# Layer 0's last tile: the work behind a recurrence, done by quarters of the tokens beside it

## The chip, the cores and the metric

The kernel runs on one NeuronCore of a Trainium2 chip. The metric is device time in microseconds (us) for one execution. The core has five engines that this text names as the profile does: PE (matmuls; PEld is its weight loads), DVE (VectorE), ACT (ScalarE), POOL (GpSimd) and SP (SyncE, which issues most DMAs). They run side by side and wait for one another on semaphores; each works its own queue in order.

## The reference, cut to what matters

Four layers, each an attention-like part and a feed-forward part, run over 8 sequences of 512 tokens with 128 channels. The change is in the first part of layer 0, a recurrence with 16 heads of 8 channels. After projections have made r, w, k, v, kk, b (and a gate g) for every token, it computes for each sequence and head:

```python
def step(S, inp):
    r_, w_, k_, v_, kk_, b_ = inp
    sab = jnp.einsum('bhvk,bhk->bhv', S, kk_)
    S = S * jnp.exp(w_)[:, :, None, :] + sab[..., None] * b_[:, :, None, :] + v_[..., None] * k_[:, :, None, :]
    y = jnp.einsum('bhvk,bhk->bhv', S, r_)
    return (S, y)
...
mu = y.mean(-1, keepdims=True)
var = ((y - mu) ** 2).mean(-1, keepdims=True)
yn = (y - mu) / jnp.sqrt(var + 0.00064) * ln_w.reshape(H, N) + ln_b.reshape(H, N)
bonus = (r4 * k4 * time_faaaa.reshape(H, N)).sum(-1, keepdims=True) * v4
out = (yn + bonus).reshape(B, T, C) * g
return out @ output.T
```

So behind the recurrence each token's eight channels of a head are normalized (mean, variance, weight and bias), a bonus is added, and the result is gated and projected.

## The kernel before, in words

Layer 0 walks the 512 tokens in four tiles of 128 (`jt` 0 to 3). In the recurrence a partition stands for one sequence and head (8 x 16 = 128). Two tokens are taken together as a pair, so a tile has `HT` = 64 pairs. The loop over `o` takes them in eight steps of `SH` = 8 pairs. In each step DVE builds `Z` (L734 to L738), then does eight time steps of ten small instructions (L747 to L759; each works on half of the value rows, so that the two halves hide each other's latency), and then multiplies the states with r into `HR` (L761 to L765). Those ten instructions depend on each other from one time step to the next.

`HR` still has to be summed over eight elements. `outputs` does this on PE: `eighths` multiplies by the identity eight times into one PSUM tile `pa` (all of it is at L364), and ACT copies the sum to its part of `Y` (L691). The call for a step stands one step later. `HR`, like `Hs`, has two buffers.

When all eight steps are done, the work behind the recurrence goes over the whole tile at once, on 128 x 1024 elements:

- DVE adds to the first token of each pair its own value times `kr` (L772, L773).
- PE sums `Y` over the eight channels (L364), and DVE makes 8 Y minus the sum (L777).
- ACT squares it into `t3` (L778), PE sums the squares (L364), ACT takes Ln and then Exp of -0.5 times that (L779, L780), which is the inverse root. ACT loads a function table ahead of each of the two.
- DVE makes V times bonus in `t3` (L781) and scales `Y` (L782), and ACT applies weight and bias, one channel at a time (eight instructions at L784).
- PE turns `Y` and `t3` together back to tokens (L796), DVE gates (L799), PE turns and projects (L804, L808) and, in the last tile, DVE multiplies by the feed-forward part and adds the residual (L813, L814).

Beside the recurrence of a tile runs other work: `coming` (projections and transposes of the next tile; there is none in the last) and `side` (the experts of the feed-forward part, which end in the last tile). In the last tile's steps 4 to 7 the feed-forward result comes back from memory (`f_d`), goes through Silu (L719), and is combined with the residual of the first three tiles (L721, L722).

The order of PE's queue is as written in the code. The order of DVE, ACT, POOL and SP is a scheduler's, which places instructions by its own estimates when the program is built. So an instruction of DVE may stand between two of the recurrence, wherever the scheduler thought that its inputs would be there.

The pool `bp` has one buffer for a name unless told otherwise, so a second tile of one name waits until the readers of the first are done.

Of the kernel before, what the change touches and what calls it, by code (L numbers as in the profile page):

```python
# [10 lines left out]
F32 = mybir.dt.float32  # L11
# [3 lines left out]
AF = mybir.ActivationFunctionType  # L15
ALU = mybir.AluOpType
# [4 lines left out]
P = 128  # L21
B = 8
T = 512
C = 128
N = B * T
NT = N // P
JT = T // P
# [45 lines left out]
def bc(ap, axis, n):  # L73

    a = ap.unsqueeze(axis)
    shape = list(a.shape)
    shape[axis] = n
    return a.to_broadcast(shape)
# [252 lines left out]
def layer0(k, x, A, at):  # L331

    nc, tc = k.nc, k.tc
# [3 lines left out]
    with ExitStack() as ctx:  # L337
# [15 lines left out]
        HT = P // 2  # L353
        s = x
# [5 lines left out]
        def eighths(src):  # L360

            ps = k.pa(src.shape[:2])
            for i in range(8):
                nc.tensor.matmul(ps, k.ident, src[:, :, i], start=(i == 0), stop=(i == 7))  # L364
            return ps
# [323 lines left out]
        def outputs(HR, y):  # L689

            nc.scalar.copy(y, eighths(HR.rearrange("p t s v n -> p (t s v) n")))  # L691

        for jt in range(JT):
            G, KE, BK, Vs, Rs, bonus, kr = ready
            coming = ahead(jt + 1) if jt + 1 < JT else iter(())
            made = None

            def go_on(n):
                nonlocal made
                for _ in range(n):  # L700
                    try:
                        next(coming)
                    except StopIteration as end:
                        made = end.value or made
            Y = bp.tile([P, P, 8], F32, name="Y")
            yp = Y.rearrange("p (t s) v -> p t s v", s=2)
            last = None
            for o in range(0, HT, SH):
                if jt == JT - 1 and o // SH >= HT // SH - JT:

                    j = o // SH - (HT // SH - JT)
                    if j < JT - 1:
                        f = fp.tile([P, B, C], F32, name=("Vt", "KNt", "Bt")[j])
                    else:
                        f = hp.tile([P, 3, 4, C], F32, name="sg").rearrange("p a b c -> p (a b) c")[:, 0:B, :]
                    old = fp.tile([P, B, C], F32, name="Gt", bufs=2)
                    nc.sync.dma_start(f, f_d.rearrange("(b j p) c -> j p b c", j=JT, p=P)[j])
                    nc.sync.dma_start(old, A["x"].rearrange("(b j p) c -> j p b c", j=JT, p=P)[j])
                    nc.scalar.activation(f, f, AF.Silu)  # L719
                    if j < JT - 1:  # L720
                        nc.vector.tensor_tensor(f, f, s_v[:, :, j, :], ALU.mult)  # L721
                        nc.vector.tensor_tensor(s_v[:, :, j, :], f, old, ALU.add)  # L722
                    else:
                        held = f, old
                next(side, None)
                go_on(3)
                if last:
                    outputs(*last)
                next(side, None)
                go_on(2)  # L730

                Z = up.tile([P, SH, 4, 8, 8], F32, name="Z", bufs=1)
                for i in range(2):
                    nc.vector.tensor_tensor(  # L734
                        Z[:, :, 3 - i], bc(Vs[:, o : o + SH, i, :], 3, 8), bc(BK[:, 1, o : o + SH, i, :], 2, 8),
                        ALU.mult,
                    )
                nc.vector.tensor_tensor(Z[:, :, 3], Z[:, :, 3], Z[:, :, 2], ALU.add)  # L738

                Hs = up.tile([P, SH, 8, 8], F32, name="Hs")  # L740
                halves = [(h, slice(h * 4, h * 4 + 4)) for h in range(2)]
                for t in range(SH):
                    prev = carry if t == 0 else Hs[:, t - 1]
                    z = Z[:, t]
                    sab = bp.tile([P, 2, 2, 4], F32, name="sab", bufs=3)
                    for h, v in halves:
                        nc.vector.tensor_tensor(  # L747
                            z[:, 0:3, v, :], bc(prev[:, v, :], 1, 3), bc(KE[:, o + t, 0:3, :], 2, 4), ALU.mult
                        )
                    for h, v in halves:  # L750
                        nc.vector.tensor_reduce(sab[:, h], z[:, 0:2, v, :], AX.X, ALU.add)
                    for h, v in halves:
                        nc.vector.tensor_tensor(
                            z[:, 0:2, v, :], bc(sab[:, h], 3, 8), bc(BK[:, 0, o + t], 2, 4), ALU.mult
                        )
                    for h, v in halves:
                        nc.vector.tensor_tensor(z[:, 0:2, v, :], z[:, 0:2, v, :], z[:, 2:4, v, :], ALU.add)
                    for h, v in halves:
                        nc.vector.tensor_tensor(Hs[:, t, v, :], z[:, 0, v, :], z[:, 1, v, :], ALU.add)  # L759
                HR = up.tile([P, SH, 2, 8, 8], F32, name="HR")  # L760
                nc.vector.tensor_tensor(HR[:, 0, 0], carry, bc(Rs[:, o, 0, :], 1, 8), ALU.mult)  # L761
                nc.vector.tensor_tensor(
                    HR[:, 1:, 0], Hs[:, 0 : SH - 1], bc(Rs[:, o + 1 : o + SH, 0, :], 2, 8), ALU.mult
                )
                nc.vector.tensor_tensor(HR[:, :, 1], Hs, bc(Rs[:, o : o + SH, 1, :], 2, 8), ALU.mult)  # L765
                carry = Hs[:, SH - 1]
                last = HR, Y[:, o * 2 : (o + SH) * 2, :].rearrange("p t v -> p (t v)")
            outputs(*last)
            go_on(40)
            ready = made  # L770
            t3 = fp.tile([P, B, C], F32, name="EWt").rearrange("p b (h n) -> p (b h) n", n=8)
            nc.vector.tensor_tensor(t3[:, 0:HT], Vs[:, :, 0, :], bc(kr, 2, 8), ALU.mult)  # L772
            nc.vector.tensor_tensor(yp[:, :, 0, :], yp[:, :, 0, :], t3[:, 0:HT], ALU.add)  # L773


            mu = bp.tile([P, P], F32, name="mu")
            nc.vector.scalar_tensor_tensor(Y, Y, 8.0, bc(eighths(Y), 2, 8), ALU.mult, ALU.subtract)  # L777
            nc.scalar.activation(t3, Y, AF.Square)  # L778
            nc.scalar.activation(mu, eighths(t3), AF.Ln, bias=k.eps_gn, scale=1.0 / 8)  # L779
            nc.scalar.activation(mu, mu, AF.Exp, scale=-0.5)  # L780
            nc.vector.tensor_tensor(t3, Vs.rearrange("p t s n -> p (t s) n"), bc(bonus, 2, 8), ALU.mult)  # L781
            nc.vector.tensor_tensor(Y, Y, bc(mu, 2, 8), ALU.mult)  # L782
            for n in range(8):
                nc.scalar.activation(  # L784
                    Y[:, :, n], Y[:, :, n], AF.Identity, scale=cn["ln_w"][:, n : n + 1], bias=cn["ln_b"][:, n : n + 1]
                )

            YT = fp.tile([P, B, C], F32, name="Rt")
            oTs = fp.tile([P, B, P], F32, name="Kt")
            yv = YT.rearrange("p b (h n) -> p n (b h)", n=8)  # L790
            gv = G.rearrange("p b (h n) -> p n (b h)", n=8)
            for n0 in range(0, 8, 4):
                ps = k.pa((P, 4, P))
                for i in range(4):
                    for src in (Y, t3):
                        nc.tensor.matmul(  # L796
                            ps[:, i, :], src[:, :, n0 + i], k.ident, start=(src is Y), stop=(src is t3)
                        )
                nc.vector.tensor_tensor(yv[:, n0 : n0 + 4, :], ps, gv[:, n0 : n0 + 4, :], ALU.mult)  # L799
            for b0 in range(0, B, 4):  # L800
                oT = oTs[:, b0 : b0 + 4, :]
                ps = k.pa((P, 4, P))
                for i in range(4):
                    nc.tensor.transpose(ps[:, i, :], YT[:, b0 + i, :], k.ident)  # L804
                nc.scalar.copy(oT, ps)
                ps = k.pa((P, 4, C))
                for i in range(4):
                    nc.tensor.matmul(ps[:, i, :], oT[:, i, :], cn["output"], start=True, stop=True)  # L808
                if jt < JT - 1:
                    nc.scalar.copy(s_v[:, b0 : b0 + 4, jt, :], ps)  # L810
                else:
                    f, old = (a[:, b0 : b0 + 4, :] for a in held)
                    nc.vector.tensor_tensor(f, ps, f, ALU.mult)  # L813
                    nc.vector.tensor_tensor(s_v[:, b0 : b0 + 4, jt, :], f, old, ALU.add)  # L814
# [1542 lines left out]
```

## Time and profile before

| | us |
|---|---|
| median of 3 runs | 3589.2 |
| lowest, highest | 3583.16, 3598.02 |
| the profiled execution | 3592.12 |
| its span, from the first to the last instruction | 3590.4 |
| mean granted PE clock, as a share of full speed | 0.861 |
| DVE busy in the span | 2323.1 |
| end of the last tile's recurrence (end of its last L765) | 838.05 |
| end of layer 0 (the last L814) | 874.98 |

A row of the timeline has start, duration, engine, line, operation, output and inputs, shapes and count; in brackets stands how long the engine had been idle before, and what ended that. A row of the windows has, for a stretch, the busy time of each engine with the number of instructions, and the clock that PE was granted. One fp32 matmul is two MATMUL records (two passes), each with its weight load. ACT's table loads have rows of their own.

### The profile page before, as it was taken

The numbers are of one execution on the slowest core, as the hardware profiler recorded it, in microseconds if no ns is written. First come the engines' busy times: TensorE is split into PE (matmuls) and PEld (weight loads), VectorE is DVE, ScalarE is ACT, GpSimd is POOL, SyncE is SP. The second block draws the span as 40 slices with busy tenths as digits, with TensorE's granted clock in tenths as the row PEclk, the third lists the DMA queues.
The fourth block names the chain that finished last, engine by engine and source line by source line (L and its number), as shares of the span: only waits on it lengthen the run. The fifth ranks groups of instructions, "written<-read, shape, count | busy, mean of one in ns | idle before, by whom it ended". The sixth has DMA issues, their size and how long they took to land.

```text
span 3590.4 us, 46304 instructions
## 1 busy us (share of the span) xinstructions
PE 2891.0 (81%) x16950; PEld 1591.5 (44%) x16950; DVE 2323.1 (65%) x6354; ACT 1793.6 (50%) x3386; POOL 733.4 (20%) x845
## 2 busy tenths in 40 slices
PE   6175868635998799698888888898789888888887
PEld 4154656534444454334434333443334444454453
DVE  7999888896583334534454554554577767777776
ACT  4173646422444355243545454455466556566655
POOL 0012131300124553211111111111112122222221
PEclk8587889766789999898999999999788888888888
DMA  4012121211001222100000000000000000000000
GB/s 121 2 30 44 32 52 32 43 49 48 1 13 35 40 42 27 45 1 1 1 1 1 1 1 1 1 1 1 21 1 1 4 1 4 4 1 7 4 1 6
DMA packets 67522, 64.59 MB, mean 18 GB/s; under 512 B 5344, under 2 KB 59616, under 8 KB 66784
## 3 DMA queue, kind: packets, MB, share of 16 engines
q1 hardware_dynamic: 39264, 42.75, 3.9%
q0 software_dynamic: 19712, 14.69, 3.1%
q10 hardware_dynamic: 8320, 4.19, 0.4%
q8 instruction: 133, 2.18, 0.2%
q14 instruction: 93, 0.76, 0.1%
HBM read 43.80 MB, written 17.83 MB: 17 GB/s over the span
## 4 chain that ended last, share of the span: by engine, by line
PE 36%; DVE 14%; ACT 10%; issue 2%; POOL 1%; DMA 0%; POOLq 0%; ACTq 0%; DVEq 0%
PE pu L1462 6%; PE ph L1443 5%; PE pu L2102 4%; DVE nm L2104 3%; PE pf L2132 2%; ACT at L2107 2%; PE pf L1511 2%; ACT at L1498 2%; ACT L1498 2%; DVE mpad L1477 1%; PE pa L1565 1%; PE pa L2145 1%; PE pu L1474 1%; PE pa L1596 1%; PE pa L2034 1%
## 5 line engine op out<-in xcount | busy, mean ns | idle before, releaser
L2107 ACT ACTIVATE at<-pu,nm 128x512 f32<-128x512 f32 x512 | 347.7, 690 | 226.8 <-DVE nm L2104 225.3
L2102 PE MATMUL pu<-qT,kT 32*128 32x512 f32 x1024 | 296.3, 740 | 79.3 <-ACT at L2107 79.1
L2104 DVE TENSOR_REDUCE nm<-pu 128x1 f32<-128x512 f32 x512 | 318.7, 680 | 39.6 <-PE pu L2102 39.2
L199 POOL TENSOR_SCALAR_AFFINE_SELECT at<-at 128x512 f32<-128x512 f32 x184 | 124.4, 676 | 1029.2 <-ACT at L1498 879.7
L1477 DVE TENSOR_REDUCE mpad<-pu 128x2 f32<-128x1024 f32 (+3 forms) x256 | 198.9, 818 | 151.1 <-PE pu L1474 151.0
L1128 ACT ACTIVATE at<-pu,rsqrt 128x1024 f32<-128x1024 f32 (+3 forms) x256 | 190.9, 792 | 188.2 <-PE pu L1123 164.1
L1443 PE MATMUL ph<-hid,f 128*128 128x512 f32 x512 | 256.9, 629 | 11.6 <-ACT hid L1444 11.5
L1498 ACT ACTIVATE at<-pu 128x1024 f32<-128x1024 f32 (+3 forms) x256 | 167.1, 701 | 163.6 <-PE pu L1462 162.5
L364 PE MATMUL pa<-HR,ident 128*128 128x128 f32 x512 | 127.4, 417 | 140.3 <-DVE HR L765 140.3
L2102 PEld LDWEIGHTS pu<-qT,kT 32*128 32x128 f32 x1024 | 100.2, 209 | 178.4 <-ACT at L2107 159.4
L364 PEld LDWEIGHTS pa<-HR,ident 128*128 128x128 f32 x512 | 112.4, 265 | 150.1 <-DVE HR L765 74.7
L2132 PE MATMUL pf<-at,va 128*32 128x512 f32 x1024 | 161.3, 708 | 11.9 <-POOL va L2119 11.9
L608 POOL DMA_INDIRECT f_d<-ys,idx x48 | 90.3, 1881 | 382.2 <-ACT ys L607 352.8
L1462 PE MATMUL pu<-kT,qT 32*128 32x512 f32 (+3 forms) x1024 | 136.2, 504 | 30.4 <-ACT at L1498 29.6
L1443 PEld LDWEIGHTS ph<-hid,f 128*128 128x128 f32 x512 | 94.8, 200 | 114.1 <-issue 90.1
L1462 PE MATMUL pu<-qT,kT 32*128 32x512 f32 (+3 forms) x1024 | 128.1, 496 | 20.3 <-DVE mpad L1477 19.9
L1123 PE MATMUL pu<-qT,kT 32*128 32x512 f32 (+3 forms) x1024 | 131.4, 519 | 5.8 <-ACT at L1128 4.9
L2119 POOL TENSOR_TENSOR va<-V,sm 128x32 f32<-128x32 f32 x128 | 34.5, 270 | 488.8 <-DVE sm L2118 428.6
L1066 POOL DMA_INDIRECT f_d<-ys,idx x64 | 103.4, 1616 | 135.1 <-DMA f_d<-ys,idx 86.1
L1498 ACT ACT_TABLE_LOAD x66 | 84.7, 1283 | 90.1 <-PE pu L1462 89.3
L1133 DVE TENSOR_TENSOR at<-at,ceiling 128x512 f32<-128x512 f32 x72 | 49.9, 694 | 106.5 <-ACT at L1128 102.5
L691 ACT COPY Y<-pa 128x128 f32<-128x128 f32 x32 | 8.4, 263 | 208.4 <-PE pa L364 208.4
(621 smaller groups left out, 6806.2 us busy)
## 6 DMA issues: line engine op xcount, KB each, us to landing
w<-in_w_dram SPq DMA_DIRECT2D x24, 512.0 KB
f_d<-zeros ACTq DMA_DIRECT2D x8, 512.0 KB, 5.7
xn_d<-xn SPq DMA_DIRECT2D x8, 512.0 KB, 3.2
w<-in_w_dram SPq DMA_DIRECT2D x16, 256.0 KB, 2.9
w<-in_w_dram SPq DMA_DIRECT2D x24, 128.0 KB, 2.1
f<-in_f_dram SPq DMA_DIRECT2D x1, 2888.0 KB
xn<-in_x_dram SPq DMA_DIRECT2D x4, 512.0 KB, 7.1
Gt<-in_x_dram SPq DMA_DIRECT2D x4, 512.0 KB, 5.0
```

Source lines behind the costliest of these rows:

```text
L199: self.nc.gpsimd.affine_select(a, a if src is None else src, pattern, ALU.is_ge, 0.0, base=0, channel_multiplier=-1)
L364: nc.tensor.matmul(ps, k.ident, src[:, :, i], start=(i == 0), stop=(i == 7))
L1123: nc.tensor.matmul(pu[:, n, 0:m], q["kT"][r, g // 2, kc * P : kc * P + P], q["qT"][r, g, kc * P :], start=True, stop=True,)
L1128: nc.scalar.activation(at_[:, i : i + 2, 0:m], pu[:, :, 0:m], AF.Square, bias=k.rsqrt2, scale=32.0**-0.5)
L1443: nc.tensor.matmul(ps, fn[n][:, c0 : c0 + P], src[:, i, :], start=(i == 0), stop=(i == 3))
L1462: self.k.nc.tensor.matmul(pu[:, n, 0:m], a[r, c0 : c0 + P], b[r, q0 : q0 + m], start=True, stop=stop)
L1477: nc.vector.tensor_reduce(top[:, i : i + 2, 16 + g % 2], pu[:, :, 0:m], AX.X, ALU.max)
L1498: nc.scalar.activation(at_[:, i : i + 2, 0:m], pu[:, :, 0:m], AF.Exp, scale=8.0**-0.5)
L2102: nc.tensor.matmul(pu, q["kT"][r, kc * P : (kc + 1) * P], q["qT"][r, g, :], start=True, stop=True)
L2104: nc.vector.tensor_reduce(nm[:, n : n + 1], pu, AX.X, ALU.max, negate=True)
L2107: nc.scalar.activation(E[:, n, :], pu, AF.Exp, bias=nm[:, w], accum_out=sm[:, w])
L2132: nc.tensor.matmul(po[i * 32 : i * 32 + 32, :], va[:, kc, c0 : c0 + 32], E[:, i, :], start=(kc == 0), stop=(kc == JT - 1))
```

## The change

In the last tile alone, the part from L772 to L784 is replaced by a generator `settle(c)` for each quarter `c` of the tile (16 pairs, 32 tokens). It has five steps, with a `yield` between them. A new quarter is begun every second step of the loop over `o`, as soon as its two `HR` have been summed; each quarter that has been begun takes one step in each further step of the loop, ahead of the sums of the last `HR`. The fourth quarter is begun after the loop, where all that is left is worked off in turns. V times bonus is written into `Vs` itself, so that L796 reads `Vs` in place of `t3`. Two tiles are new in `bp`, `square` (128 x 32 x 8) and `root` (128 x 32), with one buffer each. Tiles 0 to 2 go as before.

```diff
+            def settle(c, Y=Y, yp=yp, Vs=Vs, bonus=bonus, kr=kr):
+                pr, tk = slice(c * 16, c * 16 + 16), slice(c * 32, c * 32 + 32)
+                square = bp.tile([P, 32, 8], F32, name="square")
+                own_v = square[:, 0:16, :]
+                nc.vector.tensor_tensor(own_v, Vs[:, pr, 0, :], bc(kr[:, pr], 2, 8), ALU.mult)
+                nc.vector.tensor_tensor(yp[:, pr, 0, :], yp[:, pr, 0, :], own_v, ALU.add)
+                yield
+                y = Y[:, tk, :]
+                mean = eighths(y)
+                yield
+                nc.vector.scalar_tensor_tensor(y, y, 8.0, bc(mean, 2, 8), ALU.mult, ALU.subtract)
+                nc.scalar.activation(square, y, AF.Square)
+                v = Vs.rearrange("p t s n -> p (t s) n")[:, tk, :]
+                nc.vector.tensor_tensor(v, v, bc(bonus[:, tk], 2, 8), ALU.mult)
+                yield
+                r = bp.tile([P, 32], F32, name="root")
+                nc.scalar.activation(r, eighths(square), AF.Ln, bias=k.eps_gn, scale=1.0 / 8)
+                nc.scalar.activation(r, r, AF.Exp, scale=-0.5)
+                yield
+                nc.vector.tensor_tensor(y, y, bc(r, 2, 8), ALU.mult)
+                for n in range(8):
+                    nc.scalar.activation(
+                        y[:, :, n], y[:, :, n], AF.Identity, scale=cn["ln_w"][:, n : n + 1], bias=cn["ln_b"][:, n : n + 1]
+                    )
+                yield
+            settling = []
...
+                for w in settling:
+                    next(w, None)
                 next(side, None)
                 go_on(3)
                 if last:
                     outputs(*last)
+                    if jt == JT - 1 and o // SH % 2 == 0:
+                        settling.append(settle(o // SH // 2 - 1))
+                        next(settling[-1])
...
             outputs(*last)
+            if jt == JT - 1:
+                settling.append(settle(3))
             go_on(40)
             ready = made
+            added = Vs.rearrange("p t s n -> p (t s) n")
+            if jt == JT - 1:
+                while settling:
+                    settling = [w for w in settling if next(w, False) is not False]
+            else:
...
+                added = t3
...
-                    for src in (Y, t3):
+                    for src in (Y, added):
```

More of the change, by code (lines that the diff above doesn't have):

```diff
@@ L768, in layer0 @@
             outputs(*last)
+            if jt == JT - 1:
+                settling.append(settle(3))
             go_on(40)
             ready = made
[L771 to L786, printed above, removed]
+            added = Vs.rearrange("p t s n -> p (t s) n")
@@ new lines, in layer0 @@
+            if jt == JT - 1:
+                while settling:
+                    settling = [w for w in settling if next(w, False) is not False]
+            else:
+                t3 = fp.tile([P, B, C], F32, name="EWt").rearrange("p b (h n) -> p (b h) n", n=8)
+                nc.vector.tensor_tensor(t3[:, 0:HT], Vs[:, :, 0, :], bc(kr, 2, 8), ALU.mult)
+                nc.vector.tensor_tensor(yp[:, :, 0, :], yp[:, :, 0, :], t3[:, 0:HT], ALU.add)
+                mu = bp.tile([P, P], F32, name="mu")
+                nc.vector.scalar_tensor_tensor(Y, Y, 8.0, bc(eighths(Y), 2, 8), ALU.mult, ALU.subtract)
+                nc.scalar.activation(t3, Y, AF.Square)
+                nc.scalar.activation(mu, eighths(t3), AF.Ln, bias=k.eps_gn, scale=1.0 / 8)
+                nc.scalar.activation(mu, mu, AF.Exp, scale=-0.5)
+                nc.vector.tensor_tensor(t3, Vs.rearrange("p t s n -> p (t s) n"), bc(bonus, 2, 8), ALU.mult)
+                nc.vector.tensor_tensor(Y, Y, bc(mu, 2, 8), ALU.mult)
+                for n in range(8):
+                    nc.scalar.activation(
+                        Y[:, :, n], Y[:, :, n], AF.Identity, scale=cn["ln_w"][:, n : n + 1], bias=cn["ln_b"][:, n : n + 1]
+                    )
+                added = t3
@@ L794, in layer0 @@
                 for i in range(4):
-                    for src in (Y, t3):
+                    for src in (Y, added):
                         nc.tensor.matmul(
-                            ps[:, i, :], src[:, :, n0 + i], k.ident, start=(src is Y), stop=(src is t3)
+                            ps[:, i, :], src[:, :, n0 + i], k.ident, start=(src is Y), stop=(src is added)
                         )
```

## The prediction

> **What bounds the kernel now.** I read the page first: its span is one execution, with 1.7 us around it (3592.1 us in all, 2.9 us over the median of the three runs shown, 3589.2).
>
> ```profile
> span 3590.4 us, 46304 instructions
> ```
>
> Then busy time by stage. The last tile's recurrence runs from 731 to 838 us, what follows it up to the layer's end from 838 to 875 us.
>
> ```profile
> core 0: us, PE busy (x) PEld busy (x) DVE busy (x) ACT busy (x) POOL busy (x), PEclk, DMA share, GB/s
> 731.00:838.00 107.00, 34.75 (x163) 31.01 (x163) 103.82 (x605) 13.76 (x26) 7.26 (x8) 0.62 0.17 42
> 838.00:874.98 36.98, 25.29 (x104) 22.95 (x104) 9.69 (x17) 11.18 (x17) 3.77 (x7) 0.64 0.11 37
> ```
>
> In the first stretch VectorE (DVE) is busy 103.8 of 107 us: it is the bound, and whatever it gets to do or to wait for there lengthens the kernel. The second is a chain without a bound engine. The waits of DVE in the recurrence are two in number:
>
> ```profile
> DVE Vt L721 <- ACT Vt L719: 1.7, 1, 1.7
> DVE HR L761 <- PE pa L364: 1.1, 1, 1.1
> ```
>
> Third, the timeline of that chain (start, duration, engine, line):
>
> ```profile
> 837.36 0.69 DVE L765 TENSOR_TENSOR HR<-Hs,Rs 128x512 f32<-128x512 f32 x1
> 838.20 4.05 PE L364 MATMUL pa<-HR,ident 128*128 128x128 f32 x16 [10.11 <-DVE HR L765]
> 842.58 0.69 DVE L773 TENSOR_TENSOR Y<-Y,EWt 128x512 f32<-128x512 f32 x1 [4.53 <-ACT Y L691]
> 843.33 4.00 PE L364 MATMUL pa<-Y,ident 128*128 128x128 f32 x16 [1.08 <-DVE Y L773]
> 847.37 1.22 DVE L777 SCALAR_TENSOR_TENSOR Y<-Y,pa 128x1024 f32<-128x1024 f32 x1 [4.09 <-PE pa L364]
> 848.68 1.06 ACT L778 ACTIVATE EWt<-Y 128x1024 f32<-128x1024 f32 x1 [6.13 <-DVE Y L777]
> 849.79 4.11 PE L364 MATMUL pa<-EWt,ident 128*128 128x128 f32 x16 [2.46 <-ACT EWt L778]
> 854.32 1.28 ACT L780 ACT_TABLE_LOAD   x1
> 855.61 0.31 ACT L780 ACTIVATE mu<-mu 128x128 f32<-128x128 f32 x1
> 857.22 4.17 ACT L784 ACTIVATE Y<-Y,c 128x128 f32<-128x128 f32 x8 [1.29 <-DVE Y L782]
> 857.88 0.84 PE L796 MATMUL pa<-ident,Y 128*128 128x128 f32 x2 [3.99 <-ACT Y L784]
> ```
>
> Call T the end of L765 (838.05). L796 starts at T+19.83. Of these 19.8 us three groups of eight matmuls (x16, each fp32 matmul being two passes) take 12.2. From L796 on nothing is changed but the tile it reads, and its own pace (16 matmuls in 7.9 us) bounds it, so I carry 857.88 to the end of the layer unchanged, and the later layers too: the built order moves no SP or POOL instruction and no DMA, and the constants' load (issued at 842.28, after the HR matmuls) still lands, at about T+10.4, ahead of the DVE work that needs it.
>
> **The change part by part.** Each quarter (16 pairs, 32 tokens) has five steps: add (DVE, 2), mean (PE, 8 matmuls), center (DVE 2, ACT square 1), root (PE 8, ACT Ln and Exp with a table load each), scale (DVE 1, ACT 8). s0 to s3 are the quarters. In the built order s0, s1 and s2's center stand before the last HR; s2's root and scale and all of s3 behind it.
>
> *DVE work moved into the recurrence.* L772, 773, 777, 781 and 782 leave or go behind it; L772 (0.68 us, pitch 0.60) was in it already. An instruction's pitch there is about its elements/0.96 ns + 65 ns (L734: 512 in 0.61 us). So 128 elements cost 0.20, 256 cost 0.34. Ahead of the last HR come three each of the own-token product and its addition (0.20), three centerings, three V times bonus and two scalings (0.35): 1.2 + 2.8 = 4.0, less 0.6: **+3.4**.
>
> *DVE waits.* DVE works its queue in order, and behind a waiting instruction stands the recurrence.
>
> ```profile
> 746.80 0.43 DVE L747 TENSOR_TENSOR Z<-Hs,KE 128x96 f32<-128x96 f32 x2
> 749.67 0.27 ACT L691 COPY Y<-pa 128x128 f32<-128x128 f32 x1 [3.47 <-PE pa L364]
> 755.23 1.23 DVE L721 TENSOR_TENSOR Vt<-Vt,x 128x1024 f32<-128x1024 f32 x1 [1.68 <-ACT Vt L719]
> ```
>
> s0: its addition stands behind the L747 of 746.80, so is reached at 747.14; the copy of Y that it needs ends at 749.94: waits 2.8. Its centering stands 0.9 us of work later and needs addition (0.3) and mean (about 2.1): waits 1.35. Silu's table load now follows the square (752.96 to 753.4), so Silu can start at 754.7 instead of 754.1; L721 is reached at about 757, past Silu, and its 1.7 us wait goes. Net 2.8 + 1.35 - 1.7 = **+2.5**.
>
> s1 and s2: one buffer holds the square, so the next quarter's product waits until PE has summed the last quarter's squares, and those matmuls stand in PE's queue behind an HR group. From the undisturbed step of 823.20 (L765): PE's HR group starts at 824.03, issues 16 passes of 0.233 and is through at 827.8; the product's place (behind the first L757 half of the second time step) is reached at 828.2. The narrow sums begin at 827.8. What do eight matmuls of 32 columns take? No row has 32; the nearest narrow one is L859, 8 columns with full weights, in two windows of that line alone (stretch, its length, PE busy, PEld busy, granted clock, DMA):
>
> ```profile
> 902.00:906.00 4.00, 4.00 (x38) 4.00 (x38) 1.00 0.00 0
> 906.50:909.50 3.00, 3.00 (x16) 3.00 (x15) 0.50 0.00 0
> ```
>
> 38 passes in 4 us (0.11 each) at full clock, 16 in 3 us (0.19 to 0.21) at half. So 16 passes are 1.8 or 3.4 us, plus 0.25 to the reader. If cost went with columns, a quarter of the 4 us row would do: 1.0. The Trainium skill's "TensorE: Matmul & The Clock Gate", section "LDWEIGHTS (loading the stationary operand)", says a weight load takes its 128 columns whatever else; that speaks against quarters, and L859 agrees, so I drop 1.0 as the value. Full clock wants about 3.4 us of sustained work by the same page (section "Part 1: The HAM clock gate (the "warmup" mystery)"); here HR plus sums is 6 us of it, but single 4 us HR groups in this stage were followed by full clock only at times (mean 0.62). I take 2.4 in all, so 830.2 to 830.4: each waits **2.2** (bounds 1.6 and 3.2).
>
> s2 has one more: s1's scaling stands 0.75 us behind that product, and its table load, Ln, load and Exp (1.28 + 0.3 + 1.28 + 0.25) start only when the sums are there, as the first load now stands behind the wait: 3.1 - 0.75 = **+2.4**. (s0's scaling stands a time step later and its load ahead of the wait: covered, by one step of 1.36 us and three DVE operations; without that cover it would cost 2.4 too.) The ScalarE page ("ScalarE: Activation LUTs", "What ACT_TABLE_LOAD costs") adds a drain of 1.38 us to each load; L780's Exp starts 1.29 us after its load, so the trace decides for 1.28. By the page s2 would lose 2.8 more.
>
> Recurrence: 3.4 + 2.5 + 2.2 + 2.2 + 2.4 = **+12.7**.
>
> *The chain behind the last HR.* HR passes are issued by T+3.9 (Y's copy ends T+4.5). s2's sums follow: T+6.4. s3's product waits for them (same buffer), then its addition: T+7.0; mean, 2.4: T+9.5. Meanwhile ACT: load, Ln, load, Exp for s2, T+9.5; scaling T+9.95; eight ACTIVATEs, which shrink less than fourfold (L784 has a pitch of 0.52 at 128 strided elements, L160, with the same two operands, 2.42/6 = 0.40 at contiguous ones: about 0.35 here), 2.8: T+12.8. s3's square stands behind them: T+13.2. Sums, 3.0 after this gap: T+16.2; load, Ln, load, Exp: T+19.3; scaling, first ACTIVATE: T+20.3. Against 19.83: **+0.5** (bounds -2.5 at full clock throughout, +2 at half). The chain has four PE groups where it had three, and both loads in it wait.
>
> Sum: 12.7 + 0.5 = 13.2 on 3592.1, that is 3605 for such an execution; from the median 3602.4. I say **3603**. All bounds low: 12.7 - 1.2 - 2.5 = +9; all high: 12.7 + 2.0 + 1.5 (s0's mean at half clock) + 2 = +18.
>
> **The rivals.**
>
> Waits at their long end (slower). Mechanism: the narrow sums run at half clock, weight load by weight load, and DVE stands behind them at the four places named, with the drain of the page in s2: +18 to +21, 3607 to 3610; with one further place reached too early (s0's scaling, +2.4) 3612. For it: mean clock 0.62 in this stage, and places chosen for DVE from estimated, not measured, durations. Against it: HR and sums together are long enough to raise the clock. It decides once the DVE waits in the recurrence pass about 15 us in all (9.3 in my sum).
>
> Cover holds. DVE reaches its places when the data are there: only the 3.4 us of work, less L721's wait of 1.7, and the chain with groups at a quarter of the cost, some -4: -2 us, 3587. For it: PE is idle two thirds of the recurrence. Against it: HR's group and the square's single buffer are fixed in the order, and L859.
>
> The change does not do what it says: the chain behind the last HR is not shortened, because s2's tail lies in front of s3. That is in my sum (+0.5). Were it as short as the words promise (a quarter of each of the three groups and of the wide operations, some 9 us less), the total would be +3, 3592.
>
> **How the numbers follow.** A measurement of this kernel tells about 0.5% (18 us) from no change. My sum, 0.50; long waits, 0.38, nearly all of it slower by over 0.5%, and a little of my sum's upper end joins it; cover or a short chain, 0.12, within 0.5%. A gain of over 0.5% would need nearly the whole chain of 19.8 us to vanish at no cost to DVE: 0.03, for scatter. So faster 0.03, same 0.56, slower 0.41. Range: down to 3590 (the short chain is nearly taken in, all bounds low with scatter), up to 3616 (long waits and scatter).
>
> **What would show it.** Right: DVE idle of 1.5 to 3 us before s0's addition and before the product of s1 and s2, on ACT's copy and on PE; no wait at L721; eight ACT table loads for roots where two were; narrow groups of 1.8 to 3.7 us; L796 starting within 2.5 us of T+19.8; the last HR about 13 us later. Wrong: narrow groups near 1 us, DVE waits under 4 or over 15 us in all, or a changed time outside 731 to 875.

## The result, and the profile after

The changed kernel took 3608.28 us (median of 8 runs, 3603.49 to 3612.23), the kernel before 3590.61 us on the same chip (8 runs, 3582.65 to 3598.02). The ratio is 1.005, with a 95% interval of 1.0036 to 1.0064: 13 to 23 us slower, with the middle at the 0.5% that a measurement of this kernel tells from no change. The forecast was 3603 (3590 to 3616).

The profiled execution of the changed kernel took 3606.96 us, at a mean granted TensorE clock of 0.86 (before: 3592.12 at 0.861).

```profile
span 3605.3 us, 46556 instructions
```

Busy time by stage. The recurrence of the last tile now ends at 852 us, the layer at 889 (before: 838 and 875). Columns as in the rows of before.

```profile
core 0: us, PE busy (x) PEld busy (x) DVE busy (x) ACT busy (x) POOL busy (x), PEclk, DMA share, GB/s
731.00:852.00 121.00, 49.04 (x243) 45.14 (x243) 107.87 (x618) 26.51 (x53) 7.31 (x8) 0.62 0.15 37
852.00:889.00 37.00, 25.35 (x120) 23.92 (x120) 7.42 (x18) 14.75 (x29) 3.71 (x7) 0.67 0.10 36
```

The first stretch became 14 us longer, while DVE's busy time in it grew by only 4.1 (103.8 to 107.9). The other 10 us are idle time on the engine that bounds the stage. The second stretch is as long as before, although DVE has 2.3 us less to do in it: PE's busy time is the same and ACT's is 3.6 us higher.

Who DVE waits for in the recurrence (line, awaited engine and line, us in total, times, longest):

```profile
DVE square L713 <- PE pa L364: 4.6, 2, 3.1
DVE Y L714 <- ACT Y L691: 2.7, 1, 2.7
DVE Y L728 <- ACT root L726: 2.2, 1, 2.2
DVE HR L795 <- PE pa L364: 1.5, 1, 1.5
DVE Y L719 <- PE pa L364: 1.4, 2, 1.2
```

Before there were two waits of 1.7 and 1.1 us. Four of these five rows are steps of the quarters, 11.0 us in all (4.6, 2.7, 2.2 and 1.4, before rounding), and L721's 1.7 us is gone: +9.3. All of them end on PE or ACT. The waits of the second and the third quarter in the timeline, the two products each behind the PE group that they wait for, the scaling behind ACT's root:

```profile
789.11 3.43 PE L364 MATMUL pa<-square,ident 128*128 128x32 f32 x16
792.58 0.29 DVE L713 TENSOR_TENSOR square<-Vs,dr 128x128 f32<-128x128 f32 x1 [3.07 <-PE pa L364]
822.28 1.89 PE L364 MATMUL pa<-square,ident 128*128 128x32 f32 x16
824.28 0.29 DVE L713 TENSOR_TENSOR square<-Vs,dr 128x128 f32<-128x128 f32 x1 [1.54 <-PE pa L364]
827.41 0.43 DVE L728 TENSOR_TENSOR Y<-Y,root 128x256 f32<-128x256 f32 x1 [2.24 <-ACT root L726]
```

The chain behind the last HR, from the timeline (start, duration, engine, line, operation, output and inputs; in brackets the engine's idle time before and what ended it). T is now 851.98.

```profile
851.29 0.69 DVE L799 TENSOR_TENSOR HR<-Hs,Rs 128x512 f32<-128x512 f32 x1
852.04 4.08 PE L364 MATMUL pa<-HR,ident 128*128 128x128 f32 x16 [10.01 <-DVE HR L799]
855.94 1.89 PE L364 MATMUL pa<-square,ident 128*128 128x32 f32 x16
857.92 1.28 ACT L725 ACT_TABLE_LOAD   x1 [1.49 <-PE pa L364]
857.94 0.29 DVE L713 TENSOR_TENSOR square<-Vs,dr 128x128 f32<-128x128 f32 x1 [5.96 <-PE pa L364]
858.69 3.34 PE L364 MATMUL pa<-Y,ident 128*128 128x32 f32 x16 [0.85 <-DVE Y L714]
859.52 1.28 ACT L726 ACT_TABLE_LOAD   x1
861.53 2.78 ACT L730 ACTIVATE Y<-Y,c 128x32 f32<-128x32 f32 x8 [0.49 <-DVE Y L728]
864.22 0.40 ACT L720 ACTIVATE square<-Y 128x256 f32<-128x256 f32 x1
864.67 3.62 PE L364 MATMUL pa<-square,ident 128*128 128x32 f32 x16 [2.64 <-ACT square L720]
868.37 1.28 ACT L725 ACT_TABLE_LOAD   x1 [3.76 <-PE pa L364]
869.97 1.28 ACT L726 ACT_TABLE_LOAD   x1
871.53 0.42 DVE L728 TENSOR_TENSOR Y<-Y,root 128x256 f32<-128x256 f32 x1 [8.85 <-ACT root L726]
872.48 0.84 PE L838 MATMUL pa<-ident,Y 128*128 128x128 f32 x2 [4.19 <-ACT Y L730]
```

Read the chain by what is *not* a quarter of what it was. The wide DVE and ACT operations shrank (0.42 for 1.22, 0.40 for 1.06). The sums over eight elements took 1.89, 3.34 and 3.62 us, where the two sums of 128 columns had taken 4.0 and 4.1 (the group of 3.34 us lies beside ACT's work: the next step of the chain, the square at 864.22, waits for ACT's eight scalings and not for it). A table load is 1.28 us at any width, and now two pairs of them stand in the chain, where before the first of the one pair had lain beside PE's sums. L838 starts at T + 20.50; its counterpart L796 started at T + 19.83.

The narrow groups of PE by themselves (stretch, length, PE, PEld, DVE, ACT, POOL, granted clock, DMA):

```profile
855.90:857.80 1.90, 1.90 (x17) 1.79 (x16) 0.00 (x0) 0.27 (x1) 0.00 (x0) 1.00 0.33 57
864.70:868.30 3.60, 3.59 (x16) 3.45 (x16) 0.00 (x0) 0.00 (x0) 0.00 (x0) 0.50 0.00 0
```

Each has the same work, a sum of 32 tokens, which took 1.9 us at clock 1.00 and 3.6 at 0.50; in both PEld, the weight loads, is busy nearly throughout.

### The profile page after: what moved, and what is told of

Read it like the earlier page. It is cut to its first block, busy times and chain, and to the rows that moved or that the text cites. A ratio compares the mean times of both kernels' runs of the same rounds, so it can differ in the third digit from the quotient of the medians.

```text
span 3605.3 us, 46556 instructions
## 1 busy us (share of the span) xinstructions
PE 2906.2 (81%) x17046; PEld 1607.2 (45%) x17046; DVE 2326.0 (65%) x6369; ACT 1810.3 (50%) x3425; POOL 734.6 (20%) x845
## 4 chain that ended last, share of the span: by engine, by line
PE 37%; DVE 13%; ACT 10%; issue 3%; POOL 2%; DMA 1%; POOLq 0%; ACTq 0%; DVEq 0%
PE pu L1504 6%; PE ph L1485 5%; PE pu L2144 5%; PE pf L2174 2%; DVE nm L2146 2%; ACT at L2149 2%; PE pf L1553 2%; ACT at L1540 2%; ACT L1540 1%; DVE mpad L1519 1%; PE pa L1607 1%; PE pa L2187 1%; PE pu L1516 1%; PE pa L2076 1%; PE pa L1638 1%
## 5 line engine op out<-in xcount | busy, mean ns | idle before, releaser
L1504 PEld LDWEIGHTS pu<-kT,qT 32*128 32x128 f32 x1024 | 56.6, 188 | 123.6 <-ACT at L1540 79.7
```

The costliest lines, as they stand in the source:

```text
L1504: self.k.nc.tensor.matmul(pu[:, n, 0:m], a[r, c0 : c0 + P], b[r, q0 : q0 + m], start=True, stop=stop)
```

## The experiments

Two theories stood at first. **Waits:** beside the recurrence DVE stands still for PE and ACT, since it works its queue in order and the recurrence stands behind each waiting step; this is about 9.4 of the 13.9 us by which the last HR is late. **Work:** the 14 added instructions and their starts carry most of it. Then came rivals for where the waits and the unshortened chain have their root: the one buffer of the squares, PE's narrow groups, or ACT's table loads.

Two distances are read in each profile: from the second step's HR to the last one's (*recurrence*), and from the end of the last HR to the first matmul of the output (*tail*). What came before the second step drops out of both. Each kernel's ratio is to the kernel before on the same chip.

| kernel | recurrence | tail | both against before | DVE waits in the recurrence | ratio (95% interval) |
|---|---|---|---|---|---|
| before | 94.44 | 19.83 | | 2.8 | 1 |
| after | 108.17 | 20.50 | +14.4 | 12.7 | 1.005 (1.0036 to 1.0064) |
| e5_work_alone | 97.44 | 19.83 | +3.0 | 3.7 | 1.0011 (0.9996 to 1.0027) |
| e5b_work_in_place | 98.84 | 19.82 | +4.4 | 2.9 | 1.0009 (0.9996 to 1.0021) |
| e1_own_squares | 110.16 | 20.61 | +16.5 | 15.0 | 1.006 (1.0031 to 1.0089) |
| e2_one_table | 105.97 | 18.35 | +10.0 | 10.1 | 1.0043 (1.003 to 1.0056) |
| e3_both | 103.91 | 15.51 | +5.2 | 8.4 | 1.0034 (1.0023 to 1.0046) |
| e4_quarters_behind | 97.03 | 38.63 | +21.4 | 4.0 | 1.0063 (1.0041 to 1.0085) |
| e8_quarters_on_dve | 102.61 | 8.44 | -3.2 | 5.0 | 0.9994 (0.9983 to 1.0005) |
| e6a_sums_on_dve | 94.36 | 14.20 | -5.7 | 2.7 | 0.9991 (0.9977 to 1.0005) |
| e6b_short_tail | 94.43 | 11.23 | -8.6 | 2.8 | 0.9972 (0.9963 to 0.9982) |
| e9_quarters_on_pool | 99.92 | 5.54 | -8.4 | 4.4 | 0.9989 (0.9981 to 0.9998) |

Waits of DVE are summed from 725 us to the end of the last HR, without the wait of the tile before (1.9 to 2.0 us in each kernel). In e9 the last HR product itself took 0.46 us more, which is counted in its fourth column. There is one profile of each kernel; e6a and e6b, which leave the recurrence as it was, repeat its 94.44 us to 0.1.

### e5: the work alone

```
                 if last:
                     outputs(*last)
+                if jt == JT - 1 and o >= 2 * SH:
+                    v, w = scratch[:, 0:32, :], scratch[:, 32:64, :]
+                    nc.vector.tensor_tensor(v[:, 0:16, :], Rs[:, 0:16, 0, :], bc(kr[:, 0:16], 2, 8), ALU.mult)
+                    for i in range(1 + (o >= 6 * SH)):
+                        nc.vector.tensor_tensor(w, Rs.rearrange("p t s n -> p (t s) n")[:, 0:32, :], bc(bonus[:, 0:32], 2, 8), ALU.mult)
```

> The kernel before, with nothing of the change in it but a stand-in for the quarters' DVE work: inside the last tile's recurrence DVE also carries out 6 products of 128 elements and 8 of 256 on a scratch tile that nobody reads, so none of them waits for PE or ACT. The last HR of layer 0 started at 837.36 us before and 851.29 after (+13.93). Theory 1 (waits): 11.0 us of new DVE waits less 1.7 that went make +9.4 of this, and the quarters' own work only the rest, so this kernel's last HR is late by 3.5 to 4.6 us, and its time is +3 to +5 us (ratio 1.001). Rival (work and number of instructions): the instructions themselves, with their starts, carry most of it; then the last HR is late by 10 us or more, ratio 1.003. In both the tail behind the recurrence is unchanged: L765 to the matmul of L796's section 19.8 us.

The recurrence became 3.0 us longer, measured from the second HR, and 4.2 from the first (117.50 us against 113.27). But this was not quite the wanted experiment: the instructions read data that had been ready long, and the built order placed eight of the 14 ahead of the second HR and three more at its heels, by 747 us. So it was run again with stand-ins that can't be issued early.

### e5b: the work in its places

To e5:

```
+                    hr = last[0].rearrange("p t s v n -> p (t s v) n")
-                    nc.vector.tensor_tensor(v[:, 0:16, :], Rs[:, 0:16, 0, :], bc(kr[:, 0:16], 2, 8), ALU.mult)
+                    nc.vector.tensor_tensor(v[:, 0:16, :], hr[:, 0:16], bc(kr[:, 0:16], 2, 8), ALU.mult)
...
-                        nc.vector.tensor_tensor(w, Rs.rearrange("p t s n -> p (t s) n")[:, 0:32, :], bc(bonus[:, 0:32], 2, 8), ALU.mult)
+                        nc.vector.tensor_tensor(w, hr[:, 0:32], bc(bonus[:, 0:32], 2, 8), ALU.mult)
```

> As e5_work_alone, but the 14 stand-in products (6 of 128 elements, 8 of 256) read the HR that DVE itself wrote in the step before, so that they can't be issued earlier than in the steps where the quarters stood: in e5 they read data ready since long, and 11 of the 14 were issued before the second step's HR. Nothing that they read comes from PE or ACT. Theory 1 (waits): last step's HR minus second step's HR 97.5 to 99.5 us (before 94.44; after 108.17). Rival (work and starts in those places): 104 us or more.

+4.4 us, with DVE's waits as before (2.9 for 2.8). The fifth and the sixth step, with one product of 128 and one of 256 elements each, went from 14.16 to 14.71 us: 0.55 for the pair. (The expectation's count of 11 ahead of the second HR in e5 was eight.) The rival, which wanted 104 us or more, is out. In after, L772's 0.6 us left the recurrence, so 3.8 us of work remain; its DVE waits are 9.9 us more than before (12.7 less 2.8). Together that is 13.7, all of what the recurrence became longer by.

### e1: a buffer of its own for each quarter's squares

```
-                square = bp.tile([P, 32, 8], F32, name="square")
+                square = squares[:, tk, :]
...
+            if jt == JT - 1:
+                squares = fp.tile([P, B, C], F32, name="EWt").rearrange("p b (h n) -> p (b h) n", n=8)
```

> The kernel after, but each quarter has its own slice of a free tile for own_v and the squares, where after all four share one buffer "square" in turn. The longest single waits on DVE in after stood in front of L713, the product written into that buffer: 3.1 and 1.5 us in the recurrence, 6.0 behind it. Rival A (the shared buffer costs): with buffers of their own these go, the last HR starts 4 to 5 us earlier than after's 851.29 and the tail becomes shorter by up to 6: ratio to before 1.002 or less. Theory 1 (whatever comes next on DVE waits for the same PE and ACT results in order): the L713 waits go and reappear in front of L714, L719 and L728 in the same places, the last HR stays at 850 to 853 and the tail at 19.5 to 21 us: ratio 1.004 to 1.005, as after.

The waits at L713 are gone, and others have taken their place. Waits of DVE in the recurrence of e1:

```profile
DVE Y L719 <- PE pa L364: 5.4, 2, 4.2
DVE Y L728 <- ACT root L726: 5.2, 1, 5.2
DVE Y L714 <- ACT Y L691: 3.5, 3, 2.7
```

The product is no longer held back, but the mean stands in PE's queue behind the same groups (L719, 1.4 to 5.4) and the root behind the same sums and loads (L728, 2.2 to 5.2). In all 15.0 us of waits for 12.7. Some 1.5 us of the increase is PE's clock: the second quarter's squares took 3.43 us at 0.50 here and 1.89 at 1.00 in after, and the root at L728 stands behind them. Even without that nothing is gained. The shared buffer was where DVE waited, not why.

### e2 and e3: a root with fewer table loads

```
-                nc.scalar.activation(r, eighths(square), AF.Ln, bias=k.eps_gn, scale=1.0 / 8)
-                nc.scalar.activation(r, r, AF.Exp, scale=-0.5)
+                nc.scalar.activation(r, eighths(square), AF.Sqrt, bias=k.eps_gn, scale=1.0 / 8)
+                nc.vector.reciprocal(r, r)
```

> The kernel after, but a quarter's root is ACT's square root and DVE's reciprocal in place of logarithm and exponential on ACT, so that ACT changes its table less often: after had eight loads of 1.283 us for the four roots, before two. Theory 1: the serial ACT chains of square, load, logarithm, load, exponential are what makes DVE wait at the s0 addition (2.7) and the scaling of s1 (2.2), and what makes the tail as long as before; with four to eight loads fewer the last HR starts about 2 us earlier (849 to 850) and the tail falls from 20.5 to about 16.5: 5 to 6 us less than after, ratio to before 1.002 to 1.003. Rival B (PE's narrow groups of 1.9 to 3.7 us set it, the loads lie beside them): less than 1.5 us is won in all, ratio 1.0045 to 1.005.

> The kernel after with both edits: own squares for each quarter, and the root by square root and reciprocal. If a wait taken away only shows the next one (theory 1), the two together give more than the sum of each alone, since the L713 wait and the ACT chain stand one behind the other: last HR 847.5 to 849, tail 15 to 16.5 us, 8 to 9 us less than after, still 5 us over before (ratio 1.001 to 1.002). If rival A holds, the own squares alone give the larger part. If rival B holds, this is no better than 1.004.

Where after loaded a table eight times for its roots, these two do it once (at 790 us); no other load lies in their tail. In e2 the recurrence is 2.2 us shorter than after's, as expected; the tail fell by 2.2, not by 4. In e3 both edits together give 4.3 and 5.0. So rival A (the buffer) is out, since e1 alone gave nothing, and rival B (PE's groups alone) is out, since the loads were worth 4.4 us alone and 9.3 with the buffer. This rests on the two distances: both ratios (1.0043 and 1.0034) are worse than expected, and their intervals alone would not exclude rival B. What e2's tail lacked is on PE. The group of the third quarter's squares, behind the last HR group, in e2 and then in e3:

```profile
854.40:857.80 3.40, 3.40 (x17) 3.31 (x16) 0.00 (x0) 0.27 (x1) 0.00 (x0) 0.50 0.57 188
```

```profile
852.60:854.40 1.80, 1.80 (x18) 1.80 (x17) 0.29 (x1) 0.27 (x1) 0.00 (x0) 1.00 0.45 93
```

The same 16 passes in the same place, right behind 3.8 to 3.9 us of HR matmuls, got the half clock in e2 and the full one in e3: 1.6 us.

### e4: the quarters, all behind the recurrence

```
-                    if jt == JT - 1 and o // SH % 2 == 0:
-                        settling.append(settle(o // SH // 2 - 1))
-                        next(settling[-1])
...
-                settling.append(settle(3))
+                settling = [settle(c) for c in range(4)]
```

(With e1's own squares.)

> The quarters as in the kernel after (own squares, roots by logarithm and exponential), but all four are carried out behind the recurrence and none beside it. It prices the splitting alone. Theory 1 says that moving the quarters beside the recurrence costs about 14 us there and saves only what three quarters take behind it: here the last HR starts as before (HR of the last step minus HR of the second step 94 to 97 us, before 94.44), and the tail from the last HR's end to the matmuls of Y and the bonus product grows from 19.83 to 26 to 29 us, since PE's narrow groups (1.9 to 3.6 us each, eight of them) and ACT's eight table loads (1.28 each) stand in one row; layer end 8 to 14 us later than before, ratio 1.003 to 1.004. If the splitting itself costs nothing behind the recurrence (a quarter of the work each, overlapped between quarters), the tail is 18 to 20 and the ratio 1.000.

This was a miss, in the direction of the theory but far beyond it: the tail became 38.6 us. The loads on ACT in e4's timeline:

```profile
858.33 1.28 ACT L726 ACT_TABLE_LOAD   x1
860.39 1.28 ACT L725 ACT_TABLE_LOAD   x1 [0.54 <-DVE Y L728]
862.32 1.28 ACT L726 ACT_TABLE_LOAD   x1
864.53 1.28 ACT L725 ACT_TABLE_LOAD   x1
872.03 8.44 ACT L730 ACTIVATE Y<-Y,c 128x32 f32<-128x32 f32 x25
```

I had counted the loads, but not that ACT would be occupied almost without a gap from 858 to 880 us: eight loads in all, and 32 scalings of 32 elements (about 0.35 us each; 11.3 in all) for the 8 of 128 elements before (4.2). Splitting an ACT chain into four multiplied its fixed part by four. Beside the recurrence ACT has room for it, behind it not. The recurrence became 2.6 us longer, since the quarters' products that wait for nothing (eight, and three additions) were issued in it.

### e8: the quarters without PE

```
-                mean = eighths(y)
+                mean = bp.tile([P, 32], F32, name="mean")
+                nc.vector.tensor_reduce(mean, y, AX.X, ALU.add)
...
-                nc.scalar.activation(r, eighths(square), AF.Sqrt, bias=k.eps_gn, scale=1.0 / 8)
+                nc.vector.tensor_reduce(r, square, AX.X, ALU.add)
+                nc.scalar.activation(r, r, AF.Sqrt, bias=k.eps_gn, scale=1.0 / 8)
```

(To e3.)

> The kernel e3 (own squares, square root and reciprocal), but a quarter's two sums over eight elements are DVE reductions in place of PE matmuls against the identity, so that no quarter waits for PE. Theory 1 (DVE in the recurrence stands still for results of PE and ACT): DVE has 8 reductions of about 0.45 us more, 6 of them beside the recurrence, and yet the last HR comes earlier than in e3, HR of the last step minus HR of the second step 101 to 103 us (e3 103.91), and the tail falls from 15.5 to 8 to 10 us; layer end 1 to 4 us before that of before, ratio 0.999 to 1.001. Rival (DVE's own work is what costs): the last HR comes 3 us later than in e3, and the tail is what e3's is less the PE groups.

DVE got eight reductions more, six of them beside the recurrence, and yet the recurrence is 1.3 us shorter than in e3: 3.4 us of waits went. In the tail, no PE group stands between centring and root:

```profile
848.60 0.29 DVE L714 TENSOR_TENSOR Y<-Y,EWt 128x128 f32<-128x128 f32 x1 [4.54 <-ACT Y L691]
848.93 0.42 DVE L718 TENSOR_REDUCE mean<-Y 128x32 f32<-128x256 f32 x1
850.35 0.42 DVE L726 TENSOR_REDUCE root<-EWt 128x32 f32<-128x256 f32 x1 [0.54 <-ACT EWt L721]
852.01 2.78 ACT L732 ACTIVATE Y<-Y,c 128x32 f32<-128x32 f32 x8 [0.88 <-DVE Y L730]
```

A reduction of 256 elements on DVE is 0.42 us, where PE's group was 1.9 to 3.6 us and the trip there and back came on top. With this the quarters do shorten the tail, by 11.4 us, and the recurrence gives 8.2 of them back: no difference that can be told (0.9994).

### e6a and e6b: the short chain without quarters

The tail can be shortened where it stands. e6a, to the kernel before, in the last tile only:

```
+        def summed(src):
+            out = bp.tile([P, P], F32, name="dk")
+            nc.vector.tensor_reduce(out, src, AX.X, ALU.add)
+            return out
...
+            sums = eighths if jt < JT - 1 else summed
-            nc.vector.scalar_tensor_tensor(Y, Y, 8.0, bc(eighths(Y), 2, 8), ALU.mult, ALU.subtract)
+            nc.vector.scalar_tensor_tensor(Y, Y, 8.0, bc(sums(Y), 2, 8), ALU.mult, ALU.subtract)
...
-            nc.scalar.activation(mu, eighths(t3), AF.Ln, bias=k.eps_gn, scale=1.0 / 8)
+            nc.scalar.activation(mu, sums(t3), AF.Ln, bias=k.eps_gn, scale=1.0 / 8)
```

> The kernel before, with no quarters; in the last tile only, the two sums over eight elements (mean and squares, 128 x 1024 elements each) are DVE reductions in place of 16 matmuls of 128 columns on PE. It asks for the cheapest way to shorten the tail without touching the recurrence. Before, DVE waited 4.1 us (L777) and ACT about 5 (the sum of squares) for these. A reduction of 1024 elements should take about 1.1 to 1.3 us on DVE. Expected: the last HR as before, tail from 19.8 to 13 to 14.5 us, ratio 0.998 to 0.999. If the tail is set by ACT (square, two table loads, eight scalings) and not by the sums, it stays above 17.

e6b, in addition:

```
-            outputs(*last)
+            if jt < JT - 1:
+                outputs(*last)
+            else:
+                nc.vector.tensor_reduce(last[1], last[0].rearrange("p t s v n -> p (t s v) n"), AX.X, ALU.add)
...
+                nc.scalar.activation(mu, sums(t3), AF.Sqrt, bias=k.eps_gn, scale=1.0 / 8)
+                nc.vector.reciprocal(mu, mu)
```

> As e6a, and in the last tile also: the last eight token pairs' sum of HR over its eight elements by a DVE reduction straight into Y (before: PE matmuls and a copy by ACT), and the root by square root and DVE reciprocal in place of logarithm and exponential (one table load in place of two). Expected: tail 8 to 9.5 us, layer end 10 to 12 us earlier than before, ratio 0.9965 to 0.9975: better than before and after. If the output matmuls behind the tail or the next layer's loads are what the end waits for, the layer end moves by less than half of that.

e6a: the tail is 14.2 us, as expected; the ratio's interval (0.9977 to 1.0005) includes no change. e6b: 11.2 us, against 8 to 9.5 expected, and 0.9972, an interval clear of 1 though within the 0.5% named above: 3570.67 us, where the kernel before took 3580.2 beside it. Its tail:

```profile
836.37 1.22 DVE L777 TENSOR_REDUCE Y<-HR 128x128 f32<-128x1024 f32 x1
838.42 1.22 DVE L370 TENSOR_REDUCE dk<-Y 128x128 f32<-128x1024 f32 x1
842.07 1.28 ACT L793 ACT_TABLE_LOAD   x1
842.08 1.22 DVE L370 TENSOR_REDUCE dk<-EWt 128x128 f32<-128x1024 f32 x1 [1.18 <-ACT EWt L788]
844.66 0.94 DVE L794 RECIPROCAL mu<-mu 128x128 f32<-128x128 f32 x1
```

Three PE groups of 4 us became three reductions of 1.22, and the one load left lies beside a reduction. What the expectation missed: the product with the bonus and three small instructions stand ahead of the reciprocal in DVE's queue (it starts 0.9 us after the square root has ended, at 843.76), and a reciprocal of 128 elements takes 0.94.

### e9: the quarters on POOL

In e9 (from e8) the elementwise steps of quarters 0 to 2 go to `nc.gpsimd`, their sums to PE as in after (ACT copies them out), the root to POOL's power; the last HR is summed as in e6b. (A square root on ACT whose result nobody reads loads the last quarter's table ahead of the tail.)

```
+                eng = nc.gpsimd if c < 3 else nc.vector
-                nc.vector.tensor_tensor(yp[:, pr, 0, :], yp[:, pr, 0, :], own_v, ALU.add)
+                eng.tensor_tensor(yp[:, pr, 0, :], yp[:, pr, 0, :], own_v, ALU.add)
...
+                if c < 3:
+                    nc.scalar.activation(r, eighths(square), AF.Identity, bias=k.eps_gn, scale=1.0 / 8)
+                    nc.gpsimd.tensor_tensor(r, r, k.minus_half.to_broadcast([P, 32]), ALU.pow)
```

> Quarters beside the recurrence with DVE kept out of them: the products, additions, centring and scaling of quarters 0 to 2 are done by POOL (and their inverse root by POOL's power, their sums by PE as in after, copied out of PSUM by ACT); the last quarter, behind the recurrence, is as in e8, and the sum of the last HR over its eight elements is a DVE reduction into Y as in e6b. POOL stood idle for 87 us of the recurrence in before. Theory 1 (what costs beside the recurrence is that DVE, which bounds it, carries the quarters and waits in order for PE and ACT): with DVE free of them the recurrence is nearly as before, last HR minus second HR 95 to 98 us (before 94.44, after 108.17, e8 102.61), the tail to the output matmuls 4 to 6 us (before 19.83), the layer end after the second HR 118 to 122 us (before 131.4, e6b 123.7), ratio 0.996 to 0.997. Rival (work of another engine on the same tiles slows DVE's own instructions, or POOL is too slow for its place): the last HR minus the second is 100 us or more, and the ratio is 0.998 or more.

The tail is as expected, 5.5 us. The recurrence is not: 99.9 us, just short of the 100 that the rival wanted, and the ratio of 0.9989 is on the rival's side (0.998 or more). Waits are 1.6 us of the 5.5 by which the recurrence is longer than before. The rest shows on the timeline, where POOL's products and DVE's run side by side. POOL, then DVE, of e9:

```profile
825.90 0.73 POOL L743 TENSOR_TENSOR Y<-Y,root 128x256 f32<-128x256 f32 x1 [0.34 <-ACT root L720]
826.59 0.64 POOL L725 TENSOR_TENSOR Y<-Y,root 128x256 f32<-128x256 f32 x1
```

```profile
825.67 0.31 DVE L812 TENSOR_TENSOR Hs<-Z 128x32 f32<-128x32 f32 x2
825.90 0.85 DVE L800 TENSOR_TENSOR Z<-Hs,KE 128x96 f32<-128x96 f32 x2
826.67 0.33 DVE L804 TENSOR_REDUCE sab<-Z 128x8 f32<-128x64 f32 x2
826.93 0.53 DVE L806 TENSOR_TENSOR Z<-sab,BK 128x64 f32<-128x64 f32 x2
827.38 0.34 DVE L810 TENSOR_TENSOR Z<-Z 128x64 f32<-128x64 f32 x2
```

The pair of L800 takes 0.42 us elsewhere in this trace, and 0.85 here; the pair of L806 takes 0.35, and 0.53 here; the reduction of L804 between them is what it always is. The last HR, beside another of POOL's products, took 1.15 us for 0.69. So POOL does not come free beside a bound DVE. The Trainium skill's "SBUF — State Buffer", section "Who interferes with whom", gives the pattern: a DVE instruction with two inputs in SBUF contends with a GpSimd instruction that reads SBUF, and a reduction never does; these rows agree on both. But POOL's powers (5.4 us each), which read SBUF too, did almost nothing of this: the cost is at the products beside them. The fourth to fifth HR took 15.5 us for 14.2, without a wait of DVE. About 3.4 us of the recurrence's 5.5 go to this (the DVE instructions that overlap one of POOL's products, each against the median of its kind without POOL), 1.6 to waits, and 0.2 to the last quarter's one product that DVE carries out there; 0.3 is left over.

## Why the prediction was right, point by point

Forecast: +13.2 us on the profiled execution, 3603 for the median. Measured: +14.8 for the profiled execution, 14.1 at the end of the layer, and 17.7 between the medians (3608.28 against 3590.61). The mechanism held, and most terms with it; that the products' sum and the chain came out so close was in part luck.

- **s0 +2.5.** Addition 2.74 (2.8 forecast), centring 1.18 (1.35), L721's wait gone. Right.
- **Products of s1 and s2, 2.2 each.** 3.07 and 1.54: the sum (4.61 for 4.4) is right, but each is off by 0.7 to 0.9, and the second lies below the lower bound of 1.6. The forecast took 2.4 us for a group of squares, between its two values; one ran at half clock (3.43) and one at full (1.89). That was luck: in e1 both ran at half.
- **s1's scaling behind ACT's two loads, +2.4.** 2.24. Right. e2 shows whose it is: with the loads gone this wait is gone too.
- **Work +3.4.** The term was a little too small: e5b's 14 instructions cost 4.4, which is 3.8 with L772's 0.6 taken off. A pair of 128 and 256 elements costs 0.55 us, as the pitches of 0.20 and 0.34 had it, so the size was right in single steps; the last two steps, with two of 256 elements each, gave 2.1 instead of 1.8.
- **Not in the sum:** a wait for the x-block's DMA (0.24), s1's centring (0.27), and 0.35 more at the HR that waited before. Together 0.9.
- **Chain +0.5.** +0.67, with single errors that cancel: the sums of s2's squares were ready 0.5 us earlier (they got full clock), those of s3's squares took 3.6 us for 3.0 (half clock). s3's mean was slower too (3.34 for 2.4), but s3's square, which stood behind ACT's scalings of s2 until T + 12.2, hid that.
- **Narrow groups as long as their weight loads.** 1.9 us at full clock and 3.3 to 3.6 at half, for 1.8 and 3.4 predicted. The value that went with columns, 1.0, would have put the waits in the recurrence about 4 us lower (1.4 at each of the three places, by the forecast's sum).
- **No drain behind a table load.** The Exp of s2 starts 1.29 us after its load, and s1's scaling waited 2.24 us, not 5. The trace was the right judge there.

The rivals: "waits at their long end" needed 15 us of DVE waits and fell (9.3 in the quarters' places, 12.7 in all), although the measured median, 3608.28, lies in its 3607 to 3610 and not at the forecast's 3603. "Cover holds" fell to the same waits. "The change does not do what it says" was in the sum and is what e3 and e8 bear out: the chain was not shortened because s2's sums and s3's own four stages are made of things that don't shrink with a quarter.

What is left: medians put after 13 to 23 us over before; the layer's own landmarks give 14.1. From the end of layer 0 on, the eleven profiles with an experiment or the change took 2696.1 to 2722.5 us (before: 2715.4) without an order that I could tie to an edit. In e2 and e3 the measured ratios (+11 to +20 and +8 to +17 us) lie above their landmarks (+10.0 and +5.2), and in e9 as well (-7 to -1 us against -8.4). One profile of each can't say whether that is scatter or a cost further on; it stays open.

## What to carry to other kernels

Before work is moved beside a stage, ask which engine bounds that stage and whether the work ends up in that engine's queue: here DVE, which works in order and was 97% busy, paid for the hand-overs to PE and ACT with 9.9 us of idle time and for the work itself with 3.8, and taking away one wait showed the next one (e1). A chain of small steps is made of fixed parts (table loads, weight loads, hand-overs), so split it only after these have been removed; here removing them in place (e6b: three PE groups to DVE reductions, one table load less) gave about 10 us between the medians (8.6 by the two distances), where the split with these remedies but for the sum of the last HR (e8) gave nothing that can be measured. Behind the recurrence, where no engine is the bound, a reduction on DVE shortened the chain (e6a). Beside it DVE's extra work costs its own time (e5b), and was still cheaper than waiting for PE (e8 against e3).

## What the runs showed of the hardware

- The same narrow PE group in the same place got the half clock in one kernel (e2, 0.50, 3.4 us) and the full clock in two others (after and e3, 1.00, 1.8 to 1.9 us), each behind 3.8 to 3.9 us of HR matmuls. A chain with such a group has two lengths.
- DVE products with two inputs in SBUF took longer beside POOL products (e9: the pair of L800 0.85 us for 0.42, a single instruction of L806 up to 0.66 for 0.22), reductions did not (0.21 us each), and POOL's power, which ran 5.4 us for 32 elements, did not slow them: in the last four steps the instructions of L806 took 0.217 us without POOL and 0.216 beside the power alone, those of L800 0.252 in both (means of the trace's rows).
- A DVE reduction of 1024 elements over eight took 1.22 us; the same sum on PE took 4.0 to 4.1 us, and 1.9 to 3.6 for a quarter of it.
